# Product 7 in blocks in two more batches, and an exchange of two steps in the last one

## The chip, the cores and the metric

The kernel runs on one core of a Trainium2 chip. The metric is the device time of one execution in microseconds (us). A time is the median of several runs.

## The reference

For each of 8 batches there are two float32 inputs of 512 x 1024, x1 and x2. Three weight matrices with biases give queries and keys with 64 features and values with 512 features, for all 1024 positions:

```python
q = einsum('bcn,dc->bnd', x1, Wq) + bq
k = einsum('bcn,dc->bdn', x2, Wk) + bk[:, None]
v = einsum('bcn,dc->bdn', x2, Wv) + bv[:, None]
attn = softmax(einsum('bnd,bdm->bnm', q, k), axis=2)
out = einsum('bcm,bnm->bcn', v, attn) + x1
```

The kernel uses that (Wv x2) attn^T equals Wv (x2 attn^T). So each batch has a first large product y = x2 e^T, where e holds the exponentials that are not yet divided by their sums, and a second one, o = Wv y. The division by the sums happens on y.

## The kernel before

**The two large products.** Both are computed with a seven-product scheme for 2 x 2 blocks (Strassen-Winograd): the seven products 1 to 7 replace eight block products, at the price of sums of blocks on the left (S1 to S4) and on the right (T1 to T4) before, and sums of products behind. `first(i)` is product i of y, `second(i)` is product i of o. [...]

**Blocks inside a product.** Some products of y are split once more by the same scheme, into seven inner products on 128x256: 14 matmuls, 28 records. `inner_left` and `inner_right` compute the inner sums on VectorE (four instructions of 128x256 and four of 128x512), `multiply_onto` issues the seven inner products, and partial results are copied out of PSUM by ScalarE as the products go (`d` and `v`). For an inner product that goes on accumulating in a bank which ScalarE copies, TensorE has to wait for that copy. `complete` adds v to half of d. Product 2 is in blocks in batches 2 to 8, products 3 and 4 in all batches, product 7 in batches 3 to 6 and in batch 8. I number batches from 1; in the code `s.b` is one less. For product 7 in blocks, d is added to u5 and u6 (`multiply_7`, L471), and from there it gets into the result blocks 22 and 21.

**The order of the work.** There is no scheduler: the program's order is each engine's order. `period` is one batch; it takes along work of the next one (n): the scores of n, in halves h = 0 and 1, their maximum over keys (`fold`, then a reduction over partitions on GpSimd, `highest`, L221), the subtraction of the maximum (`lower`, VectorE, L249), the exponential (ScalarE, L253) and the sum of the exponentials (`copy_first`, then `add_tile` as accumulating DMAs from GpSimd's queue; `total` and `shares` reduce over partitions, L226, and take the reciprocal). Projections of the batches after are in it too: queries of the one after next (nn) between the scores of half 0 and product 5, keys of nn between the scores of half 1 and product 4. Batch 7 has no nn, and batch 8 no n.

**Hooks.** `multiply` and `multiply_onto` take hooks: work of ScalarE that is issued right behind the copy of a given inner product.

**PSUM.** Banks a0, a1 and c0, c1 hold running results; the pool `ps_s` has two tiles (tag `sc`), which the scores, projections and the two inner banks of a product in blocks (`chain` and `third`) use in turn. A new user waits until the previous user of its tile was copied out.

**The rest of a batch.** `evict_y` takes a result block of y out of PSUM in two steps: 1 adds the partial sum u, 2 multiplies by the reciprocal sums. Block 12 is taken out by `evict_3` (L483) behind product 3, block 21 behind product 4 (L502, L507 and L505). `sum_y` makes T1 to T4 of y. `second(2)` reads block 21 and `second(7)` writes over the banks that `evict_o` of block 11 (L548) reads. T4 of the exponentials is summed on VectorE in batches 1 and 2 (L262), later by a ScalarE copy and accumulating DMAs from GpSimd's queue (L278, L280).

## Time and profile before

| | |
|---|---|
| median of 3 runs | 693.22 us (693.14 to 693.31) |
| profiled execution | 693.62 us, span 691.8 us |
| granted TensorE clock | 1.00 |
| TensorE (PE) busy | 682.8 us, 99% of the span |
| VectorE (DVE) busy | 628.9 us, 91% |
| ScalarE (ACT) busy | 276.1 us, 40% |
| GpSimd (POOL) busy | 193.5 us, 28% |
| batch 2 on TensorE | 119.81 to 204.28 us of the span |
| batch 6 on TensorE | 455.25 to 538.92 us |
| batch 7 on TensorE | 538.92 to 616.77 us |

The profile is of one execution; its span begins and ends with the first and last instruction, and the execution's own time is 1.8 us longer. PEld is the loading of weights into TensorE, beside the matmuls. In a timeline row the first number is the start in us, the second the time from the first to the last instruction of the row, and the brackets tell how long the engine was idle before it and what ended that. Matmuls overlap, so the distance between their starts tells more than their duration.

### The profile page before, as it was taken

Reading aid. Unit: us, or ns where it says so; the run is one execution under the profiler, and the core shown is the slowest. Engines: PE = TensorE matmul, PEld = TensorE weight load, DVE = VectorE, ACT = ScalarE, POOL = GpSimd, SP = SyncE. Lnnn points to the kernel's source line nnn. Section 1 sums busy time; section 2 is a strip of 40 time slices with the busy share of each in tenths; the row PEclk is TensorE's granted clock in tenths of the full one; section 3 lists DMA queues with packets and bytes.
Section 4 is the critical chain, followed back from the end, with each engine's and each line's share of the span. In section 5 each row is a group of like instructions: output and inputs, shape, how many; then the busy total and the mean of one; then the engine's idle time right before and its main releaser. Section 6 shows DMA issues by size and latency. Waiting matters only on the chain.

```text
span 691.8 us, 6647 instructions
## 1 busy us (share of the span) xinstructions
PE 682.8 (99%) x2248; PEld 364.2 (53%) x2248; DVE 628.9 (91%) x809; ACT 276.1 (40%) x439; POOL 193.5 (28%) x147
## 2 busy tenths in 40 slices
PE   9999999999999999999999999999999999999997
PEld 5333554535545565455644566454754545545753
DVE  1999999988999889998999989999799988999785
ACT  2733353146233552345432454424544245243220
POOL 0123113522423223242142321623223232323000
PEclk9999999999999999999999999999999999999999
DMA  9676256954569754786628867198642864268303
GB/s 304 258 214 238 65 182 130 255 161 79 183 114 235 199 106 153 150 231 181 135 111 180 230 181 187 42 198 215 167 92 38 207 166 76 62 148 223 87 0 122
DMA packets 44723, 109.05 MB, mean 158 GB/s; under 512 B 4880, under 2 KB 7184, under 8 KB 44688
## 3 DMA queue, kind: packets, MB, share of 16 engines
q1 hardware_dynamic: 25856, 70.13, 30.1%
q0 software_dynamic: 17424, 36.25, 29.7%
q10 hardware_dynamic: 1408, 2.23, 1.0%
q8 instruction: 18, 0.29, 0.2%
q14 instruction: 17, 0.14, 0.1%
HBM read 72.62 MB, written 16.81 MB: 129 GB/s over the span
## 4 chain that ended last, share of the span: by engine, by line
PE 93%; DMA 3%; DVE 1%; SPq 1%; ACT 1%; issue 0%; DVEq 0%
PE ps_ya L321 24%; PE ps_i L374 17%; PE ps_oa L321 16%; PE ps_oc L321 12%; PE ps_s L191 6%; PE ps_yc L374 5%; PE ps_q L149 4%; PE ps_k L149 3%; PE ps_yc L321 3%; PE ps_ya L374 3%; DMA a<-in_x2T_dram 1%; DMA x_in_x_dram<-in_x_dram 1%; DMA x_head<-in_x_dram 1%; PE ps_sc L191 1%; PE ps_sa L191 1%; DVE aS L110 0%
## 5 line engine op out<-in xcount | busy, mean ns | idle before, releaser
L321 PE MATMUL ps_ya<-eT,aS 128*128 128x512 f32 x256 | 113.1, 595 | 0.0
L332 ACT COPY uy<-ps_ya 128x512 f32<-128x512 f32 x48 | 28.1, 588 | 139.6 <-PE ps_ya L321 126.7
L249 DVE TENSOR_TENSOR e<-e,top 128x1024 f32<-128x1024 f32 x60 | 70.5, 1228 | 11.0 <-POOL top L221 11.0
L321 PEld LDWEIGHTS ps_ya<-eT,aS 128*128 128x128 f32 x256 | 48.0, 190 | 60.9 <-issue 58.5
L253 ACT ACTIVATE e<-e 128x1024 f32<-128x1024 f32 x60 | 62.9, 1059 | 38.6 <-DVE e L249 37.1
L221 POOL PARTITION_ALL_REDUCE top<-max x16 | 32.8, 2052 | 150.8 <-DVE max L215 78.9
L226 POOL PARTITION_ALL_REDUCE den<-sum x16 | 63.4, 3961 | 40.8 <-DVE sum L215 35.8
L321 PE MATMUL ps_oa<-yT,w_S 128*128 128x512 f32 x128 | 57.6, 593 | 0.0
L321 PE MATMUL ps_oc<-y,w 128*128 128x512 f32 x128 | 57.6, 593 | 0.0
L321 PE MATMUL ps_ya<-e,a 128*128 128x512 f32 x128 | 56.3, 593 | 0.3 <-ACT e L244 0.3
L200 ACT COPY e<-ps_s 128x1024 f32<-128x1024 f32 x46 | 45.7, 1027 | 19.3 <-PE ps_s L191 17.5
L332 ACT COPY uo<-ps_oa 128x512 f32<-128x512 f32 x48 | 27.6, 584 | 54.2 <-PE ps_oa L321 44.9
L383 ACT COPY d<-ps_i 128x256 f32<-128x256 f32 x84 | 29.3, 374 | 47.7 <-PE ps_i L374 47.2
L191 PE MATMUL ps_s<-q,k 64*128 64x512 f32 x188 | 47.3, 608 | 0.8 <-ACT q L590 0.8
L551 POOL DMA_DIRECT2D uo<-in_x_dram x21 | 24.9, 1186 | 79.2 <-DVE uo L548 79.2
L555 POOL DMA_DIRECT2D sum<-e x21 | 25.7, 1222 | 66.5 <-DMA sum<-e 37.0
L321 PEld LDWEIGHTS ps_ya<-e,a 128*128 128x128 f32 x128 | 24.2, 190 | 31.3 <-issue 29.6
L321 PEld LDWEIGHTS ps_oa<-yT,w_S 128*128 128x128 f32 x128 | 24.2, 190 | 30.8 <-issue 29.9
L321 PEld LDWEIGHTS ps_oc<-y,w 128*128 128x128 f32 x128 | 24.1, 190 | 31.0 <-issue 28.9
L211 DVE TENSOR_TENSOR max<-max,e 128x1024 f32<-128x1024 f32 x30 | 36.8, 1225 | 3.0
L507 DVE TENSOR_TENSOR y<-y,den 128x512 f32<-128x512 f32 x54 | 33.8, 683 | 0.0
L238 POOL DMA_DIRECT2D den<-row x16 | 8.9, 557 | 79.0 <-DMA row<-few 73.2
(142 smaller groups left out, 1291.4 us busy)
## 6 DMA issues: line engine op xcount, KB each, us to landing
x_in_x_dram<-in_x_dram SPq DMA_DIRECT2D x60, 512.0 KB, 5.9
a<-in_x2T_dram SPq DMA_DIRECT2D x32, 512.0 KB, 7.1
sum<-e POOLq DMA_DIRECT2D x21, 512.0 KB, 5.2
uo<-in_x_dram POOLq DMA_DIRECT2D x21, 512.0 KB, 6.5
out_dram<-uo SPq DMA_DIRECT2D x21, 512.0 KB, 5.1
eT<-eT POOLq DMA_DIRECT2D x12, 512.0 KB, 6.5
den<-row POOLq DMA_DIRECT2D x16, 256.0 KB, 3.6
r<-in_x_dram POOLq DMA_DIRECT2D x7, 512.0 KB, 8.6
```

The costliest lines, as they stand in the source:

```text
L149: nc.tensor.matmul(ps[r, :], w_sb[:, c, :], s.x[:, c, ts(h, H)], start=(c == 0), stop=(c == CT - 1),)
L191: nc.tensor.matmul(ps[g], s.k[r, ts(i, P)], s.q[r, ts(h, H)], start=True, stop=True)
L200: nc.scalar.copy(e[:, :, i, :], whole)
L211: nc.vector.tensor_tensor(f, e[:, :, 0, :] if i == 1 else f, e[:, :, i, :], op)
L221: nc.gpsimd.partition_all_reduce(s.top[h], s.mx[h][:, 0, :], P, ReduceOp.max)
L226: nc.gpsimd.partition_all_reduce(s.den[h], s.mx[h][:, 0, :], P, ReduceOp.add)
L249: nc.vector.tensor_tensor(e, e, top, ALU.subtract)
L253: nc.scalar.activation(e, e, AF.Exp)
L321: nc.tensor.matmul(ps[:, n], left[ka][:, k, ts(j, P)], right[kb][:, k, n], start=opens and k == 0, stop=i in (2, 3, 4) and k == n_k - 1, s ...
L332: nc.scalar.copy(s.tmp[i][:, j, :], ps)
L374: nc.tensor.matmul(ps, s.inner[i][ka][:, k, :], s.inner[i, "t"][kb][:, k, :], start=opens and k == 0, stop=z in (2, 3, 4) and k == MH // 2 ...
L507: nc.vector.tensor_tensor(y[:, j, :], y[:, j, :], rden, ALU.mult)
```

## The change

Product 7 of y is computed in blocks in batches 2 and 7 too, so in all batches but the first (`seven`). With that, batch 2 gets T4 by a copy and DMAs, like batches 3 to 8.

In batches 2, 7 and 8 (`late`) `first(5)` carries no exponential. In batches 2 and 7 the exponentials of the next batch and the copy that begins their sum are hooked on later inner products: exponential 0 and the copy on inner products 6 and 5 of product 7, exponentials 1 to 3 with their accumulating DMAs on 1, 6 and 5 of product 3. The left and right inner sums of product 4 go behind `evict_3` in these two batches. In batch 7 the right inner sums of product 3 (`nn` is missing there) go ahead of the four subtractions of the maximum. In batch 8 the right inner sums of product 4 go ahead of `evict_3`, which takes block 12 out.

```diff
     def sum_t4(s):
 
         s.t["T4"] = t4 = sb.tile([P, MH, H], F32, tag="eT4", name=f"eT4_{s.b}")
-        if s.b < 2:
+        if s.b == 0:
             sum_e(s, "T4")
             return
...
-        seven = 2 <= s.b < B - 2 or n is None
+        seven = s.b > 0
+        late = s.b in (1, B - 2) or n is None
...
         first(6)
-        if s.b == 1:
-            inner_right(s, 4, s.t["T4"], "eT2")
         if s.b:
             inner_left(s, 3, s.a["S4"], "aI3")
-        if s.b > 1 and not seven:
-            inner_left(s, 4, s.a["22"], "a12")
         if seven:
             inner_left(s, 7, s.a["S3"], "yT4")
             inner_right(s, 7, s.t["T3"], "yT1", "yT2")
...
         if seven:
             hooks = [{}, {}]
+            if late:
+                first(5)
+            if not nn:
+                inner_right(s, 3, s.t["22"], "eT1")
             if n:
                 for i in range(MH):
                     lower(n, 0, i)
-                hooks = [
-                    {
-                        1: lambda: copy_first(n, 0),
-                        6: lambda: add_exponential(1),
-                        5: lambda: add_exponential(2),
-                    },
-                    {6: lambda: add_exponential(3)},
+                steps = [
+                    lambda: exponential(n, 0, 0),
+                    lambda: copy_first(n, 0),
+                    lambda: add_exponential(1),
+                    lambda: add_exponential(2),
+                    lambda: add_exponential(3),
                 ]
-            first(5, (lambda: exponential(n, 0, 0)) if n else None)
-            inner_right(s, 3, s.t["22"], "eT1")
-            inner_left(s, 4, s.a["22"], "a12")
+                if late:
+                    hooks = [dict(zip((6, 5), steps)), dict(zip((1, 6, 5), steps[2:]))]
+                else:
+                    hooks = [dict(zip((1, 6, 5), steps[1:])), {6: steps[4]}]
+            if not late:
+                first(5, steps[0])
+            if nn:
+                inner_right(s, 3, s.t["22"], "eT1")
+            if not (late and n):
+                inner_left(s, 4, s.a["22"], "a12")
             add_7 = multiply_7(s, hooks[0])
             add_7()
             evict_3 = multiply_3(s, hooks[1])
             evict_y(s, "22", (1,))
-            evict_3()
+            if n:
+                evict_3()
+            if late and n:
+                inner_left(s, 4, s.a["22"], "a12")
             inner_right(s, 4, s.t["T4"], "eT2")
+            if not n:
+                evict_3()
         else:
             first(5)
...
         for k in ("11", "12", "22"):
             evict_y(s, k, (2,))
-        if s.b == 1:
-            inner_left(s, 4, s.a["22"], "a12")
```

## The prediction

> **What bounds the kernel now.** I read the page first (busy times, then the chain of work that ended last), then the waits of TensorE, then the busy times by batch, and then the timeline of batches 2, 6, 7 and 8, engine by engine.

> ```profile
> PE 682.8 (99%) x2248; PEld 364.2 (53%) x2248; DVE 628.9 (91%) x809; ACT 276.1 (40%) x439; POOL 193.5 (28%) x147
> ...
> PE 93%; DMA 3%; DVE 1%; SPq 1%; ACT 1%; issue 0%; DVEq 0%
> ```

> TensorE sets the time: what it saves counts in full, and so does each new wait. VectorE is near full too. The only long wait of TensorE after the head, from its list of waits, is in batch 8:

> ```profile
> PE ps_i L374 <- DVE eI4eT L367: 2.3, 1, 2.3
> ```

> By batch (6, then 7; PE first, DVE in the third column) VectorE's work is as long as TensorE's whole batch:

> ```profile
> 455.25:538.92 83.67, 83.67 (x282) 45.75 (x281) 78.45 (x103) 35.78 (x57) 24.69 (x19) 1.00 0.61 144
> 538.92:616.77 77.85, 77.56 (x238) 41.43 (x237) 72.92 (x91) 31.74 (x49) 24.71 (x19) 1.00 0.53 121
> ```

> Batch 6 has product 7 in blocks already: 78.45 us of VectorE. Batch 7, with no projections behind it, gives only 77.85 us; so the question is where VectorE's lag meets TensorE.

> **TensorE's saving: 2 x 0.83 us.** From the chain in order of time, a product in blocks (product 2) and product 7 of batch 7 as it is:

> ```profile
> 545.79 6.04 PE ps_i L374 x28
> ...
> 569.40 6.87 PE ps_yc L321 x16
> ```

> 28 records of 128x256 take 6.04 us (0.216 each), 16 of 128x512 take 6.87 (0.429 each): half the columns cost half. 6.87 - 6.04 = 0.83 per batch, -1.66 in all. [...]

> **Batch 8: -2.45 us.** The timeline there:

> ```profile
> 654.49 0.69 DVE L452 TENSOR_TENSOR d<-d,v 128x512 f32<-128x512 f32 x1 [1.16 <-ACT d L383]
> 655.29 1.29 DVE L483 TENSOR_TENSOR y<-ps_ya,d 128x512 f32<-128x512 f32 x2
> 655.34 1.03 PE L374 MATMUL ps_i<-eT,a 128*128 128x256 f32 x4
> ...
> 656.49 0.68 DVE L367 TENSOR_TENSOR eI4eT<-eT 128x512 f32<-128x512 f32 x1
> 657.21 0.69 DVE L367 TENSOR_TENSOR eI4eT<-eI4eT,eT 128x512 f32<-128x512 f32 x1
> 657.82 0.68 DVE L367 TENSOR_TENSOR eI4eT<-eT 128x512 f32<-128x512 f32 x1
> ...
> 658.65 1.97 PE L374 MATMUL ps_i<-eI4eT,aI 128*128 128x256 f32 x8 [2.28 <-DVE eI4eT L367]
> ```

> The second inner product of product 4 needs the third sum (end 658.50); TensorE goes on 0.15 us later. Without the wait it would start one step of 0.86 after 655.34, at 656.20: 2.45 us lost. With the four sums ahead of block 12 they begin at 653.33, in VectorE's idle 1.16 us, and the third ends at 655.34, 0.7 us before it is needed. What is late next: block 12 leaves the bank at about 657.9 (656.58 + 2.53 - 1.16), and `second(1)` writes there from 661.4 on; block 21's first half was scaled 2.2 us ahead of `second(2)` (668.52 and 670.77) and VectorE gains only 1.16 of the 2.45, so 0.9 us is left. All of it is gained.

> **Batch 7: VectorE's queue.** Start-to-start costs from batch 6's rows: four right inner sums 2.53, four left 1.47, four subtractions 4.55, `complete` and the two sums with d 3.00, block 22 0.93, `complete` and block 12 2.00, seven scalings 3.68, T1 and T2 2.40, the maximum of half 1 4.52, block 21's sums 2.65, taking it out 0.93, its first scaling 0.68. The rows of batch 7 that matter:

> ```profile
> 568.47 4.63 DVE L249 TENSOR_TENSOR e<-e,top 128x1024 f32<-128x1024 f32 x4 [1.83 <-POOL top L221]
> ...
> 581.30 0.69 DVE L452 TENSOR_TENSOR d<-d,v 128x512 f32<-128x512 f32 x1 [1.93 <-ACT d L383]
> ...
> 594.43 2.13 DVE L462 TENSOR_TENSOR uy<-uy,d 128x512 f32<-128x512 f32 x2
> ```

> The two idle times are all the air that VectorE has. The third row is two instructions that take 1.29 in batch 8, where no reduction runs: 0.84 more beside one of GpSimd.

> Ahead of the maximum four left sums change places with four others; product 7's right sums add 2.53, so it ends at 569.00 instead of 566.47. The right sums of product 3 wait for `first(5)` (569.43) and run beside the reduction: 2.53 + 0.84, to 572.80. From there nothing lets VectorE rest: 4.55 + 3.00 + 0.93 + 2.00 + 1.47 + 2.53 + 3.68 + 2.40 + 4.52 + 2.65 + 0.93 + 0.68 = 29.34, so block 21's first half is scaled at 602.14 (before: 598.36).

> TensorE's first wait in this batch is a copy: exponential 0 waits for its subtraction (574.01), runs 1.06 and holds the two copies of inner product 5 (0.65) until 575.77; product 3 needs that tile at 569.24 + 6.04 = 575.28. That is +0.49. The other hooks hide behind later inner products: their subtractions are 1 us or more ahead. Product 4's sums are there at 586.8, as its second inner product comes up at 586.95 behind the score copies. Then `second(2)`, which started at 599.44, is due at 599.44 - 0.83 + 0.49 = 599.10, and gets its operand at 602.14 + 0.15 = 602.29: +3.19. Batch 7 in sum: -0.83 + 0.49 + 3.19 = +2.85. VectorE's remaining lag against TensorE, 3.78 - 2.85 = 0.9 us, ends in batch 8, where it waited 1.14 us for `first(5)`.

> The 0.84 is bounded by 0 (no slowing: +2.01 for the batch) and by the whole reduction (1.78 us from 569.2, so sums only from 571.0: +3.6); I take the measured row. [...]

> **Batch 2: the same queue with more air.** VectorE loses T4's sums (2.25) and adds 1.47 + 2.53 ahead of the maximum, while product 4's 2.53 goes behind it: the maximum ends at 151.85, 0.78 earlier, and the subtractions run 153.85 to 158.40. Product 7 starts at 153.71 as before; copies and exponentials find their data 2 us early, no wait. VectorE goes on: 2.53 (right sums of product 3, the third 0.2 us ahead of its use), 3.00, 0.93, to 164.86; block 12 to 166.98 (its copies end 164.98); 1.47 + 2.53 + 3.68 + 2.40 + 4.52 + 2.65 + 0.93, so block 21 is out at 185.16, and scaled first at 185.84, in time for `second(2)` at 186.12. Then scalings, the sum's fold, T3 and T4, two subtractions (1.27 + 0.61 + 1.13 + 3.18 + 2.27) to 193.62, and block 11 leaves bank c0 at 194.36 instead of 192.75.

> ```profile
> 192.01 1.40 DVE L548 SCALAR_TENSOR_TENSOR uo<-ps_oc,bv_sb,uo 128x512 f32<-128x512 f32 x2
> ...
> 193.81 1.45 PE L321 MATMUL ps_oc<-y,w 128*128 128x512 f32 x3
> ```

> `second(7)` overwrites that bank, due at 192.98, and starts at 194.51: +1.53. Batch 2: -0.83 + 1.53 = +0.70. The lag left, 1.61 - 0.70 = 0.9, ends in batch 3, where VectorE idled 0.53 and 1.16 us for copies.

> T4's two copies take 2.0 us of ScalarE, which is idle 4.79 us at 131.4 to 136.2. Its two DMAs stand in GpSimd's queue behind the issue at 141.07 and ahead of the reduction at 151.9; batch 6's issues took 1.8 us and such a transfer 6.5 (the page's DMA issues), so it lands near 151, 17 us before its use. The accumulating DMAs of the exponentials' sums begin within 1 us of where they did, 5.3 us apart, and end some 6 us before the fold. These cost nothing; if T4 were late, product 4 at 173 would be.

> **Sum.** +0.70 + 2.85 - 2.45 = +1.1. The profiled execution took 693.62, so 694.7; the median is 0.40 under it, so 694.3. Gains of 4.1 us stand against 5.2 us of new waits.

> **Rivals.**
> - Faster: the waits stay small, because part of VectorE's queue is not where I put it, and the gains of 4.11 show. The point: block 21 of batch 7 scaled by 599, or TensorE not waiting there over 0.7 us. For it: 4 us of idle in each batch. Against it: the two idle times of batch 7 are already counted. With no wait at all: 689.1.
> - Slower: GpSimd's reduction holds VectorE for its whole length in batch 7, so product 3's sums start at 571.3 (2.15 us, as reductions beside a busy VectorE take): end 573.83, 1.03 later, and all the queue with it: 695.3. It decides at 0.3 us more than I count. For it: 2.39 for a 0.42 instruction at 467.61, beside the longer reduction. Against it: 0.84 in row 594.43.
> - The exchange in batch 8 does nothing, as another operand of product 4 comes last: 696.8. Against it: the row names the sums, and inner product 1 ran through.

> **Chances.** A difference of 0.2% (1.4 us) is about what a measurement of this kernel can tell. My case 0.58, with a range of its own of 693.3 to 695.5 (0.42 of it within 1.4 us, 0.16 slower); the faster rival 0.15 (0.13 faster); the slower one 0.20 and the idle exchange 0.07, 0.26 of this slower. Together: faster 0.13, same 0.45, slower 0.42. The range 691.5 to 696.2 leaves out the full gain and the idle exchange.

> **What would show it.** 28 records of 6.04 us for product 7 in batches 2 and 7; no wait for eI4eT in batch 8; a wait at `second(2)` of batch 7 for block 21 of about 3 us, and one at `second(7)` of batch 2 for L548 of 1.5. If both waits are short, I have VectorE's queue wrong; a wait of product 3 or 4 of over 1 us on exponentials or inner sums would mean that the late hooks cost more than I see.

## The result, and the profile after

Run beside the kernel before, the changed kernel takes 696.24 us (median of 22 runs, 693.35 to 698.39) against 693.91 us (22 runs, 693.14 to 697.17). The ratio is 1.0027, with a 95% interval of 1.0015 to 1.0038: slower by about 1.9 us. On the 693.22 us shown above, this ratio makes 695.1 us, where 694.3 was forecast. Of the 66 runs of the kernel before that are on record, one, beside the runs e1 to e4 below, took 1212.64 us at a mean clock of 0.556 and is left out.

The profiled execution took 697.72 us (before: 693.62), with a span of 695.9 us. From its page, busy times and the chain by engine:

```profile
PE 684.8 (98%) x2272; PEld 370.5 (53%) x2272; DVE 634.9 (91%) x833; ACT 281.0 (40%) x451; POOL 203.0 (29%) x149
...
PE 89%; DVE 4%; DMA 4%; issue 1%; POOL 1%; ACT 0%; DVEq 0%; POOLq 0%; ACTq 0%
```

TensorE has 24 more matmul records: in one piece product 7 is 8 matmuls, which the profile counts as 16 records, in blocks it is 14 matmuls and 28 records, and two products were changed. Half columns should have taken off 1.7 us, yet its busy time rose by 2.0: that is the first hint that some matmuls ran slower than before. Its share of the chain fell from 93 to 89%, so there are new waits on it. TensorE's list of waits names them (total, times, longest, in us):

```profile
PE ps_i L374 <- ACT d L383: 3.2, 1, 3.2
...
PE ps_oc L321 <- DVE uo L548: 0.8, 1, 0.8
```

The row of eI4eT of 2.3 us is gone, the wait on L548 is there, shorter than forecast, and the longest is one that the forecast did not have. Each batch measured from the first matmul of its `first(1)` to the next one's (batch 8 to the last matmul) gives the balance:

| us | start of batch 1 | 1 | 2 | 3 to 6 | 7 | 8 |
|---|---|---|---|---|---|---|
| before | 24.96 | 94.69 | 84.46 | 334.65 | 77.85 | 71.50 |
| after | 26.89 | 94.13 | 85.49 | 334.59 | 82.13 | 68.98 |
| difference | +1.93 | -0.56 | +1.03 | -0.06 | +4.28 | -2.52 |
| forecast | 0 | 0 | +0.70 | 0 | +2.85 | -2.45 |

The first two columns belong to this execution (+1.93 and -0.56 of its 4.1 us): no changed line runs there, and the runs below start batch 1 at 24.9 to 25.4. The other three make +2.8 where +1.1 was forecast.

**Batch 8** went as forecast. Its timeline:

```profile
661.21 0.68 DVE L367 TENSOR_TENSOR eI4eT<-eT 128x512 f32<-128x512 f32 x1
...
661.98 1.03 PE L374 MATMUL ps_i<-eT,a 128*128 128x256 f32 x4
662.41 0.69 DVE L452 TENSOR_TENSOR d<-d,v 128x512 f32<-128x512 f32 x1
662.84 1.89 PE L374 MATMUL ps_i<-eI4eT,aI 128*128 128x256 f32 x8
```

The third sum ends at 661.89, 0.95 us ahead of the second inner product, which follows the first after one step of 0.86 and waits for nothing. Block 12's `complete` now stands behind the sums.

**Batch 7** did not. Its timeline around product 4 (the number in brackets is idle time before, and its releaser):

```profile
592.17 0.42 DVE L505 TENSOR_TENSOR y<-uy,den 128x256 f32<-128x256 f32 x1
...
592.68 0.37 ACT L383 COPY d<-ps_i 128x256 f32<-128x256 f32 x1 [3.91 <-DVE y L505]
...
593.11 1.63 PE L374 MATMUL ps_i<-eI4eT,aI 128*128 128x256 f32 x4 [3.15 <-ACT d L383]
594.52 1.91 PE L374 MATMUL ps_yc<-eT,a 128*128 128x256 f32 x4
...
603.01 0.68 DVE L507 TENSOR_TENSOR y<-y,den 128x512 f32<-128x512 f32 x1
...
606.08 3.60 PE L321 MATMUL ps_oc<-y,w 128*128 128x512 f32 x8
```

`second(2)`, the last row, waits for nothing: block 21's first half was scaled at 603.69. TensorE had stopped earlier, at product 4's third inner product, which goes on accumulating in a PSUM tile that ScalarE had not yet copied to d; and that copy stood 3.91 us for the last scaling of block 22. `multiply_4` puts d into the buffer "u5", which holds block 22's unscaled part until L505 has read it. VectorE's lag, which the forecast followed to `second(2)`, meets TensorE here first.

The second thing is in the next two matmul rows: four records take 1.63 and 1.91 us instead of 1.03. By stretches (length, busy time of PE, PEld, DVE, ACT and POOL, granted clock, DMA share, GB/s): batch 7, then the 3.4 us behind the wait.

```profile
541.10:623.23 82.13, 78.69 (x249) 44.81 (x248) 76.89 (x104) 33.29 (x54) 25.88 (x19) 0.98 0.53 120
593.60:597.02 3.42, 3.42 (x9) 2.71 (x9) 3.28 (x4) 0.37 (x1) 0.00 (x0) 0.50 0.81 139
```

The clock granted to TensorE was 0.50 for 3.42 us right behind the wait; work of 1.71 us took 3.42. The third inner product starts 4.29 us after the second (588.82) instead of one step of 0.86, so the wait delays it by 3.43; the five steps behind it take 6.10 us, where they take 4.43 in the run e1 below: 1.67 more. Together -0.83 + 3.43 + 1.67 = +4.27, of 4.28.

**Batch 2** in the same view:

```profile
176.04 0.42 DVE L505 TENSOR_TENSOR y<-uy,den 128x256 f32<-128x256 f32 x1
...
176.54 0.37 ACT L383 COPY d<-ps_i 128x256 f32<-128x256 f32 x1 [0.89 <-DVE y L505]
...
195.33 1.40 DVE L548 SCALAR_TENSOR_TENSOR uo<-ps_oc,bv_sb,uo 128x512 f32<-128x512 f32 x2
196.12 3.70 PE L321 MATMUL ps_oc<-y,w 128*128 128x512 f32 x8 [0.84 <-DVE uo L548]
```

Here too the d copy waits for block 22's scaling, which costs TensorE about 0.4 us at product 4; about 0.3 goes at product 3 for its third inner sum, and `second(7)` starts 1.0 us late: -0.83 + 0.3 + 0.4 + 1.0 = +0.9, measured +1.03.

### The profile page after: what moved, and what is told of

It reads as the page before. It is cut to its first block, busy times and chain, and to the rows that moved or that the text cites. A ratio compares the mean times of both kernels' runs of the same rounds, so it can differ in the third digit from the quotient of the medians.

```text
span 695.9 us, 6738 instructions
## 1 busy us (share of the span) xinstructions
PE 684.8 (98%) x2272; PEld 370.5 (53%) x2272; DVE 634.9 (91%) x833; ACT 281.0 (40%) x451; POOL 203.0 (29%) x149
## 4 chain that ended last, share of the span: by engine, by line
PE 89%; DVE 4%; DMA 4%; issue 1%; POOL 1%; ACT 0%; DVEq 0%; POOLq 0%; ACTq 0%
PE ps_ya L321 24%; PE ps_i L374 16%; PE ps_oa L321 14%; PE ps_oc L321 11%; PE ps_s L191 5%; PE ps_yc L374 5%; PE ps_q L149 4%; PE ps_k L149 3%; DMA sum<-e 3%; PE ps_ya L374 2%; PE ps_yc L321 2%; DVE e L249 1%; PE ps_q L586 1%; PE ps_sc L191 1%; DMA x_head<-in_x_dram 1%
## 5 line engine op out<-in xcount | busy, mean ns | idle before, releaser
L321 PE MATMUL ps_ya<-eT,aS 128*128 128x512 f32 x256 | 113.1, 595 | 0.0
L226 POOL PARTITION_ALL_REDUCE den<-sum x16 | 70.9, 4428 | 40.4 <-DVE sum L215 35.4
L321 PEld LDWEIGHTS ps_ya<-eT,aS 128*128 128x128 f32 x256 | 47.9, 190 | 60.9 <-issue 58.5
L249 DVE TENSOR_TENSOR e<-e,top 128x1024 f32<-128x1024 f32 x60 | 72.0, 1253 | 9.1 <-POOL top L221 9.1
L221 POOL PARTITION_ALL_REDUCE top<-max x16 | 32.9, 2054 | 157.4 <-DVE max L215 81.2
L321 PE MATMUL ps_oc<-y,w 128*128 128x512 f32 x128 | 57.7, 593 | 0.8 <-DVE uo L548 0.8
L321 PE MATMUL ps_oa<-yT,w_S 128*128 128x512 f32 x128 | 57.6, 593 | 0.0
L321 PE MATMUL ps_ya<-e,a 128*128 128x512 f32 x128 | 56.3, 593 | 0.3 <-ACT e L244 0.3
L383 ACT COPY d<-ps_i 128x256 f32<-128x256 f32 x92 | 32.0, 374 | 52.3 <-PE ps_i L374 46.6
L321 PEld LDWEIGHTS ps_oc<-y,w 128*128 128x128 f32 x128 | 24.2, 190 | 31.9 <-issue 29.2
L321 PEld LDWEIGHTS ps_ya<-e,a 128*128 128x128 f32 x128 | 24.2, 190 | 31.3 <-issue 29.6
L321 PEld LDWEIGHTS ps_oa<-yT,w_S 128*128 128x128 f32 x128 | 24.2, 190 | 30.8 <-issue 30.1
L548 DVE SCALAR_TENSOR_TENSOR uo<-ps_oc,bv_sb,uo 128x512 f32<-128x512 f32 x42 | 29.6, 743 | 3.2 <-PE ps_oc L321 3.2
```

Of the source, the lines that this page charges most:

```text
L221: nc.gpsimd.partition_all_reduce(s.top[h], s.mx[h][:, 0, :], P, ReduceOp.max)
L226: nc.gpsimd.partition_all_reduce(s.den[h], s.mx[h][:, 0, :], P, ReduceOp.add)
L249: nc.vector.tensor_tensor(e, e, top, ALU.subtract)
L321: nc.tensor.matmul(ps[:, n], left[ka][:, k, ts(j, P)], right[kb][:, k, n], start=opens and k == 0, stop=i in (2, 3, 4) and k == n_k - 1, s ...
L383: nc.scalar.copy(copy, ps)
```

## The experiments

The theory after the result: (1) batch 7's loss is the buffer u5 plus VectorE's lag behind it, (2) a wait of about 3 us also costs clock, (3) batch 8's exchange is a gain by itself. The rival: batch 7 loses because VectorE's queue is too long wherever the wait shows.

**Another buffer for product 4 (e1_d4_own).** The d copy goes into "i2", free by then, in all batches but 1 and 8:

```diff
-        d, complete = multiply_onto(s, 4, "u5" if s.b < B - 1 else "a21", "r")
+        d, complete = multiply_onto(s, 4, "u5" if s.b == 0 else "i2" if s.b < B - 1 else "a21", "r")
```

> The changed kernel, with product 4's partial results d in a buffer of their own (that of product 2's, free by then) in batches 2 to 7, instead of u5's. My theory: in batch 7 the copy of inner product 1 of product 4 waits for the last scaling of block 22, which reads u5; that costs TensorE 3.3 us, and the halved clock behind it 1.7 us more. Then both go, and the wait that I had forecast comes out: second(2) for block 21, 2.8 us. Batch 7 on TensorE 82.1 - 5.0 + 2.8 = 79.9 us, batch 2 shorter by 0.3 and then longer at second(7), so about the same 85.5. Rival A: the wait at second(2) lets the clock drop too: batch 7 81.6. Rival B: the lag of VectorE was only felt through that buffer: batch 7 77.1.

Measured: 695.5 us (10 runs, 693.27 to 699.96), ratio 1.0028 (1.0006 to 1.0051), as the change itself. Batch 2 took 83.99 (85.5 expected), batch 7 81.60, as rival A has it. In batch 7 the wait moved (timeline, then the 3.4 us from 600.66 on):

```profile
600.27 0.68 DVE L507 TENSOR_TENSOR y<-y,den 128x512 f32<-128x512 f32 x1
...
601.09 4.29 PE L321 MATMUL ps_oc<-y,w 128*128 128x512 f32 x6 [2.86 <-DVE y L507]
```

```profile
600.66:604.07 3.41, 2.98 (x4) 1.46 (x5) 3.41 (x6) 1.07 (x2) 1.76 (x1) 0.50 0.00 0
```

With the buffer out of the way, `second(2)` waits 2.86 us for block 21, and here too there is a stretch at half clock; it begins 0.43 us before the wait ends. So the buffer only set where the lag shows; the rival is right for batch 7. This wait, which puts `second(2)` 3.02 us behind its place, is the forecast's 3.19. The clock doesn't always fall: of the 10 runs five have a mean clock of 1.0 and five of 0.995 to 0.998.

**Only the exchange of batch 8 (e2_swap).** The kernel before, with this alone:

```diff
-            evict_3()
+            if n:
+                evict_3()
...
             inner_right(s, 4, s.t["T4"], "eT2")
+            if not n:
+                evict_3()
```

> The kernel before with one part of the change: the exchange in batch 8. If the part is worth what the two traces say, batch 8 up to the end takes 72.5 us instead of 75.0, no wait of product 4 for its right sums, and the time is 690.8 us. Rival: the exchange only moves VectorE's lag to second(2) of batch 8: 75.0 us and 693.2.

Measured: 690.99 us (10 runs, 690.44 to 693.77), ratio 0.9956 (0.9942 to 0.9969): about 3.1 us faster than before, and the fastest of all versions. Batch 8 took 68.98 to its last matmul, as in the changed kernel, and 72.7 to the end of the span, where 72.5 was expected. Batch 7 took 77.85 as before. Batch 2 took 85.09 where the profile of before has 84.46: no line of it is changed here, so batch 2 differs by 0.6 us from one execution to another by itself. The gain is larger than the 2.52 us of batch 8, and the runs of before suggest why. The 24 beside this run fall into two groups, 12 at 693.1 to 693.9 us with a mean granted clock of 0.999 or 1.0, and 12 at 694.7 to 696.1 us, of which ten have 0.997 or 0.998. A stretch of 3.4 us at half clock takes 0.0025 off the mean and costs 1.7 us, which is the distance of the groups. So the wait of batch 8, the only long one of before, seems to drop the clock in some executions and not in others; the profiled one was without. None of the 10 runs with the exchange has less than 0.999, and none of the 22 of e3 and e7 below, which have it too. So the lower clocks go with the missing exchange; that it was this wait that dropped the clock is argued from the clocks, as no trace of a slower run of before exists.

**The change without its batch 7 (e3_b7_whole).**

```diff
-        seven = s.b > 0
-        late = s.b in (1, B - 2) or n is None
+        seven = s.b > 0 and s.b != B - 2
+        late = s.b == 1 or n is None
...
+        if s.b == B - 2:
+            inner_left(s, 4, s.a["22"], "a12")
```

> The changed kernel with batch 7 as it was (product 7 whole, exponentials early, product 4's sums as before); batches 2 and 8 stay changed. If batch 7 carries the loss and batch 2 loses 1.0 us: batch 7 77.9 us, batch 2 85.5, batch 8 72.5, time 691.7 us. Rival: batch 2's lag goes on into later batches and batch 7 alone is not the loss: over 693.

Measured: 692.27 us (10 runs, 691.03 to 694.01), ratio 0.9974 (0.9959 to 0.9989). Batch 7 is back at 77.85, with batch 2 at 85.50 and batch 8 at 68.98. So the parts add up: batch 7 alone turns a gain of 1.8 us into a loss of 1.9, and the two differ by 3.7; batch 2 takes about 1.3 us off the gain of the exchange (692.27 against 690.99, though the intervals of the two ratios overlap). What makes up the change inside batch 7, the blocks, the later exponentials and the order of the sums, was not run apart.

**What the clock costs: matmuls inside the wait (e4_warm, e5_warm_a1).** Seven matmuls whose result nobody reads (14 records, 3 us) are put ahead of product 4's third inner product in batch 7 of the changed kernel, in the first try into the free half of the second inner product's tile, in the second (shown) into the bank a1:

```diff
+            if i == 4 and z == 7 and s.b == B - 2:
+                spare = ps_a.tile([P, H], F32, tag="a1", name="ps_spare")
+                for _ in range(7):
+                    nc.tensor.matmul(
+                        spare[:, left], s.a["22"][:, 0, 0:P], s.t["T4"][:, 0, left], start=True, stop=True
+                    )
```

> The changed kernel with seven matmuls more of 128x256 (3.0 us, results unused, in the free half of a PSUM tile) in batch 7, behind the second inner product of product 4, where TensorE waits 3.3 us. They shorten no wait. If the halved clock (593.6 to 597.0 us in the changed kernel) comes from that idle time, it stays at full speed and batch 7 takes 82.1 - 1.7 = 80.4 us. Rival: the slow stretch has another cause (operands, or a limit on the chip that comes at random): batch 7 stays at 82.1 or gets longer.

> The changed kernel with seven matmuls more of 128x256 (results unused) in batch 7 behind the second inner product of product 4, as in the try before it, but into bank a1, which nobody holds then, so that they run while TensorE would wait 3.3 us. If the slow stretch is the clock's answer to the idle time, the clock stays at 1.0 there and batch 7 takes 82.1 - 1.7 = 80.4 us. Rival: it stays at 82.1 or more.

The first does not settle it: the added matmuls had to wait for the copy of the second inner product (v), which stands behind the d copy, so they stood in the wait themselves (3.47 us) and then ran for the most part at half clock (4.98 us for the 14 records); batch 7 took 85.48 and the run 699.52 us. The second did what it should; its timeline and the stretch from 586 to 600:

```profile
587.25 3.19 PE L450 MATMUL ps_spare<-eT,a 128*128 128x256 f32 x14
590.97 1.13 PE L374 MATMUL ps_i<-eI4eT,aI 128*128 128x256 f32 x4 [0.53 <-ACT d L383]
```

```profile
586.00:600.00 14.00, 13.16 (x49) 9.34 (x50) 13.72 (x19) 3.05 (x8) 3.33 (x2) 1.00 0.49 101
```

The useless work covers the wait, the clock stays at 1.00, and batch 7 takes 81.08 us (1.05 less than in the changed kernel, and 0.7 more than the 80.4 expected); the one run gave 694.14 us. The third inner product is as late as before, 3.79 us behind its place instead of 3.43, but the five steps behind it take 4.42 us instead of 6.10. So 1.68 us is the price of standing still, beside the wait itself. (2) rests on one execution of each; by chance alone a full clock is rare, as 21 of the 22 runs of the changed kernel have a mean clock under 0.999, and the last section says which stretches were slowed in all nine traces.

**Taking work from ahead of block 21 (e6_late_max).** On top of e1, in batch 7 the maximum of half 1 (4.5 us of VectorE) moves behind `second(2)`:

```diff
-            for i in range(1, MH):
-                fold(n, 1, i, "max", ALU.max)
-            highest(n, 1)
+            if nn:
+                max_1()
...
+            max_1()
```

> The changed kernel with product 4's d in a buffer of its own (batches 2 to 7), and in batch 7 the maximum of half 1 (4.52 us of VectorE) behind second(2) and block 11 instead of ahead of block 21. If VectorE's queue up to block 21 is what cost batch 7 its time, block 21 comes 4.5 us earlier, TensorE's 3.0 us at second(2) and the clock's 1.7 us go, and batch 7 takes 77.0 us, 0.83 less than before the change; batch 8 stays at 69.0 on TensorE, and the time is about 689.4 us, less than before and than the exchange alone. Rival: the late maximum makes the exponentials of half 1 late, and product 6 of batch 8 waits for its right sums: batch 8 at 71 or more and no gain over 690.8.

Measured: 697.57 us (8 runs, 696.03 to 699.33), ratio 1.0045 (1.003 to 1.0061), the slowest but for e4's one run, with 83.08 us for batch 7. Block 21 came 5.5 us earlier (594.76) and `second(2)` waited for nothing, as expected, but the expectation of 77.0 us was wrong, and the rival had the wrong place. TensorE's list of waits and the timeline:

```profile
PE ps_oa L321 <- ACT uo L332: 4.3, 1, 4.3
```

```profile
610.11 2.19 ACT L253 ACTIVATE e<-e 128x1024 f32<-128x1024 f32 x2 [11.22 <-DVE e L249]
612.20 1.05 ACT L332 COPY uo<-ps_oa 128x512 f32<-128x512 f32 x2
```

ScalarE's exponentials of half 1 now wait 11 us for their subtractions, behind the late maximum; and `second(5)`'s copies stand behind them in ScalarE's queue, so `second(3)` finds its bank full for 4.3 us. The lag was passed on to another queue, and the clock was halved there too (0.50 from 612.51 to 615.93).

**Batch 2 with the other buffer and batch 7 as before (e7_b2_own).** e3's edit and e1's line together.

> The changed kernel with batch 7 as it was before, and product 4's d in a buffer of its own in batches 2 to 6: batch 2's part alone without its wait at product 4. Batch 2 84.0 us as in the run with the own buffer (85.5 with u5), if that run's missing wait at second(7) came from the buffer; the time about 690.3. Rival: that wait went only because GpSimd's reduction happened to fall later, and comes back: 85.0 to 85.2 and 691.3.

Measured: 692.52 us (12 runs, 690.67 to 694.11), ratio 0.9974 (0.9961 to 0.9987), no better than e3, with 86.46 us for batch 2 where e1 had 83.99 with the same code in that batch. Two places differ. Here a reciprocal on VectorE waited for a DMA, which e1 does not show, and its queue ran 0.98 us later from there on:

```profile
139.01 0.18 DVE L234 RECIPROCAL few<-few 128x4 f32<-128x4 f32 x1 [0.89 <-DMA few<-den]
```

And at the end of the batch, the sum of yT and GpSimd's reduction meet. In e7:

```profile
188.17 4.14 POOL L226 PARTITION_ALL_REDUCE den<-sum  x1 [3.29 <-DVE sum L215]
...
189.14 3.26 DVE L262 TENSOR_TENSOR yT<-y,yT 128x1024 f32<-128x1024 f32 x1
```

In e1:

```profile
187.25 7.55 POOL L226 PARTITION_ALL_REDUCE den<-sum  x1 [3.29 <-DVE sum L215]
...
188.21 1.21 DVE L262 TENSOR_TENSOR yT<-y,yT 128x1024 f32<-128x1024 f32 x1
```

Either VectorE's sum takes 2.05 us longer (e7) or GpSimd's reduction 3.41 us longer (e1). The waits of TensorE in batch 2 follow: 1.1 us for eI3eT and 1.2 at `second(7)` in e7, 0.1 and none in e1. So with this buffer the change makes batch 2 between 0.5 us shorter and 2.0 us longer than the 84.46 of before, from one execution to another (e6, with the same code in batch 2, has 84.10); with u5 it was -0.1 (e5, 84.38) to +1.0 (e3, 85.50).

The other traces settle the rival. In all nine, batch 2 has one of these two pairs of times. Of the seven with the changed batch 2, the four in which VectorE is held (the changed kernel, e3, e4, e7) have the wait at `second(7)`, and the three in which GpSimd is held (e1, e5, e6) have none. As e5 is without it with u5, and e7 has it with the own buffer, the buffer does not decide it. The buffer's own share is the 0.4 us at product 4, which the four traces with u5 have and the three with the own buffer have not. What decides which engine is held stays open.

## Why the prediction was right or wrong

- **TensorE's saving, 0.83 per batch: right.** Product 7 of batch 2 stands in the chain of after as 28 records from 155.26 to 161.30, 6.04 us, against 6.87 in one piece.
- **Batch 8, -2.45: right**, in size (-2.52) and in mechanism; the next late things (block 12's bank, block 21) cost nothing, as worked out. What it did not see is that this wait probably cost some 1.7 us more in other executions (10 of the 24 beside e2).
- **Batch 7, +2.85 against +4.28: the step that failed is "TensorE's first wait in this batch is a copy".** Three terms of it differ. The 0.49 of exponential 0 did not come: product 3's copies were on time, because the subtraction that exponential 0 waits for came 0.8 us earlier than forecast. The 0.84 did not come: VectorE arrived some 1.6 us earlier, so the reduction had run (569.98 to 571.76) before product 3's sums began at 571.79, and the air went into waiting for `first(5)` instead:

```profile
569.98 1.78 POOL L221 PARTITION_ALL_REDUCE top<-max  x1 [9.38 <-DVE few L234]
...
571.79 0.69 DVE L367 TENSOR_TENSOR eI3eT<-e 128x512 f32<-128x512 f32 x1 [1.82 <-PE ps_ya L321]
```

  The queue behind it was summed well: block 21's first half was scaled 62.59 us into the batch, against 63.38 forecast with the 0.84 and 62.54 without. But ScalarE's copies were followed only to what they read; that product 4's d is written into block 22's old buffer, so that L505 must come first, was not looked up. That put the wait (3.43 where 3.19 was forecast at `second(2)`) at another place. Without the buffer, e1 shows the forecast's place with 2.86.
- **The missing term is the clock.** The sum had nothing for it: 1.67 us of the 4.28. Without it the forecast would have been off by 0.2 there (2.61 against 2.85), its misses partly cancelling. That the whole came out near the forecast (695.1 us against 694.3) is in part luck: a wait at a place that was not foreseen stood in for the one that was, and the clock's price was not in the sum.
- **Batch 2, +0.70 against +1.03: right in sign, its terms mis-sized.** 1.53 at `second(7)` measured 1.0, and product 3 and 4 waited 0.7 together, where the forecast had no wait ("the third 0.2 us ahead of its use" left no room, and u5 again). With the batch scattered over 2.5 us between e1 and e7, and by 0.6 between two traces of unchanged code, the nearness of the two numbers shows little.
- **The rivals.** The reduction did not hold product 3's sums in batch 7 (they began 0.03 us after it, because `first(5)` ended then), and the exchange was not idle; the slower end came by the clock, which none of them had. The faster one would have needed VectorE's lag to be air, and e1 showed a wait of 2.86 with product 4's buffer out of the way.

## What to carry to other kernels

A copy has two sides: look up who last reads the buffer that it writes, not only who makes what it reads. Price a new stop of TensorE like those here (2.45 to 4.4 us) with a chance of 1.7 us on top, and a removed one likewise; the last section says what the chance hangs on. When a change bundles a removed wait with work for an engine that has no air left, run the parts alone: here the exchange of two steps gains 3.1 us (690.99 us), and the products in blocks take it back.

## What the runs showed of the hardware

- **A stop of TensorE is paid twice, and not each time.** Stops of 3.0 (e1), 3.4 (after), 3.8 (e4) and 4.4 us (e6) came with 3.41 us at a granted clock of 0.50 in the profiled executions, and it seems that one of 2.45 us did in some of the executions of before (10 of the 24 beside e2); over all runs the mean clock is under 0.999 in 21 of 22 of after, and in 5 of 10 of e1. What comes ahead of the halved stretch is shown by the 3.41 us before it, in after and in e1 (columns as above: PE's busy time stands behind the length, the clock third from the end):

```profile
590.18:593.60 3.42, 0.49 (x2) 0.47 (x3) 3.42 (x6) 0.65 (x2) 1.18 (x1) 1.00 0.18 31
```

```profile
597.25:600.66 3.41, 0.99 (x3) 0.16 (x1) 3.41 (x6) 0.00 (x0) 1.77 (x1) 1.00 0.00 0
```

  TensorE was busy for 0.49 and 0.99 us of them, and for 1.14 and 0 us of the like in e4 and e6: a stretch need not be empty for the next one to be slowed.

```profile
654.05:657.47 3.42, 2.31 (x11) 1.70 (x9) 2.84 (x5) 0.78 (x3) 0.00 (x0) 1.00 0.01 2
657.47:660.88 3.41, 2.23 (x11) 2.01 (x11) 3.41 (x7) 0.60 (x2) 0.00 (x0) 1.00 0.00 0
```

  Each half left TensorE busy for 2.2 us or more, and the clock stayed at 1.00. Wholly inside one stretch this wait of 2.28 us would leave 1.1 us (an estimate, 3.41 - 2.28), as little as in e4, where the clock fell. So whether a stop of 2 to 3 us is punished can hang on where it falls, which would explain why it differs from run to run. In the nine traces a stretch with 1.14 us or less of matmuls, once full clock was reached, was always followed by half clock, and one with 1.80 us (e5, from 686.82) or more never; where the limit lies between them was not tried.
- **VectorE's sum and GpSimd's reduction slow one another, and either can lose:** 3.26 beside 4.14 us, or 1.21 beside 7.55, for the same two instructions of the same code; in batch 2 the first in six traces and the second in three. In e7 the sum, at 3.26 us, ends 0.09 us after the reduction; in e1, at 1.21, it began and ended inside the reduction's 7.55 us.
